# Cross-attention stack on one core: steps taken in pairs, a double piece after each, projection through a score pair, norm factors through DRAM

## The chip, the core and the metric

The kernel runs on one core of one Trainium2 chip. The time is the device time of one execution in microseconds. Before the change it was 5190.16 us, the median of three runs (5169.63 to 5191.87).

## What is computed

Four cross-attention layers, one after another, update the same 2048 rows of 256 numbers (`x`) from 1601 context rows of 512 (`ctx`). Layers 0, 2 and 3 are "masked": 16 heads of 64, with a bias on a few key columns that depends on the query row. Layer 1 is "grouped": 16 query heads of 16, four key heads, and an RMS norm ahead of it. All is float32.

```python
# masked layer
q, k, v = x @ Wq, ctx @ Wk, ctx @ Wv            # 16 heads of 64
logits = einsum('bhqd,bhkd->bhqk', q, k) * 64 ** -0.5
col_bias[:, token_indices_A] = -20 * (1 - mask_A)[:, None]
col_bias[:, token_indices_B] = -20 * (1 - mask_B)[:, None]
probs = softmax(logits + col_bias)
x = einsum('bhqk,bhkd->bhqd', probs, v) @ Wo + bo + x
# grouped layer
xn = x * rsqrt(mean(x * x) + 1e-5) * norm_w
q, k, v = xn @ wq, ctx @ wk, ctx @ wv           # 16 query heads, 4 key/value heads of 16
x = x + softmax(q k^T / 4) v @ wo
```

## The kernel before

**Blocks, units, chunks.** A masked layer has 8 blocks of two heads, the grouped layer 4 blocks of four heads that share one key head. A block is worked through for four query tiles of 512 rows; one query tile of one block is a unit, so there are 96 masked and 16 grouped units. The 1601 keys are cut into 13 chunks (`NT`): twelve of 128 and one of 65, the tail, in which the keys with a bias have been gathered.

**A masked unit.** For each chunk `masked_scores` (L662) multiplies the keys of both heads with the queries: two products of 64 rows, side by side in the array, into a score pair in PSUM (two banks). ScalarE copies the pair to an SBUF tile `p` (L680), VectorE keeps a running maximum `top` (L685, L683 for the second chunk). After the 13th chunk `maxima` (L721) transposes `top` on TensorE (L728), reduces it (L729), writes the result to DRAM and reads it back onto all partitions (`spread`, two DMAs of `on_all_partitions`, L630); `maxima_spread` (L741) copies it into the PSUM tile `b` (L744). Then, chunk by chunk, VectorE subtracts it (L749), ScalarE takes the exponential (L754), GpSimd adds it up over the chunks (L757, L759), and `values` (L779) multiplies by the values of both heads, into 64 columns each, and adds up in the one bank `po` (L794). After the last chunk `po` is copied to `oT` (L799). `denominators` (L805) transposes the sums (L815), reduces (L819), inverts (L820) and sends them over DRAM onto all partitions (`by`); `divide` (L834) multiplies `oT` by it on GpSimd; `project` (L837) multiplies by the output weights, one half of the 256 columns at a time, through the bank `pm`, and adds to `xs` (L846; L844 in a layer's last block, with the bias).

**PSUM** has eight banks: `po`, `pm` (one buffer each), two score pairs, and the pair `b`. In the grouped layer the three pairs are six single banks `t`.

**Pipeline by steps.** A step scores one chunk of one unit. The exponentials of a unit begin `DELAY` = 4 steps after its last score, its values follow one step (`LAG`) behind them. `p` has `NP` = 21 buffers. The loop at L978 writes out each step in order: subtraction (L749) of the older unit, scores and copy and maximum of the younger, exponential, (at the first step of a unit) the maxima of the one before, values of the older. The order of the program's instructions on TensorE, ScalarE and VectorE is fixed as written (L1055 to L1061); SyncE issues the DMAs in its own order, with waits.

**Pieces.** Work for later units and blocks is put between steps. `Pieces.step` (L902) first runs what is due at the step: the queries of the next unit (two halves of 256 columns, due at its steps 7 and 8, L428), `denominators` 2 steps, `divide` 5 steps, the two halves of `project` 7 and 8 steps after the last values of the unit. Then, as far as a credit of TensorE time allows, it takes pieces from a queue: the keys and the values of the next block, one chunk a piece (L398 and L409), each four products over the 512 context columns into `pm`, and a copy by ScalarE (L407, L418). The context comes as slices of two chunks (`context_slice`, L237).

**Grouped layer.** Row maxima are found from scores with the queries as columns (L699), the scores are computed a second time (L764) and go into the exponential; four heads of 32 rows at a time. `norm_factors` (L580) computes the RMS factors of a query tile and sends them through a DRAM tile onto all partitions of a constant tile `factors`, which the queries are multiplied by (L561).

Of the kernel before, what the change touches and what calls it, by code (L numbers as in the profile page):

```python
# [18 lines left out]
P = 128  # L19
QB = 512  # L20
# [5 lines left out]
Piece = namedtuple("Piece", "run cost")  # L26
# [7 lines left out]
def tile_cross_attention_stack(ctx: ExitStack, tc: tile.TileContext, t: dict, out: bass.AP):  # L34

# [43 lines left out]
    NP = 21  # L79
# [156 lines left out]

    def context_slice(c, held):  # L237

        a = TCH[c][0]
        n = sum(m for _, m in TCH[c : c + 2])  # L240
        ct = work.tile([P, NCT, 2 * P], FP, name="ct", bufs=3)
        nc.sync.dma_start(out=ct[:, :, :n], in_=ctxT_dram[:, :, a : a + n])
        for d in range(len(TCH[c : c + 2])):
            held[c + d] = lambda k, d=d: ct[:, k, d * P : (d + 1) * P]

    def first_context_slice(i):
# [21 lines left out]
        return lambda c, k: tiles[k // 2][:, k % 2, TCH[c][0] - a0 : TCH[c][0] - a0 + P]  # L268
# [93 lines left out]
    factors = const.tile([P, NB, QB], FP, name="factors")  # L362
# [5 lines left out]
    class Masked:  # L368
# [26 lines left out]
        def projections(self, u):  # L395


            def keys(c, ct):  # L398
                if u.kT is None:
                    u.kT = heads.tile([P, T], FP, name="kT")  # L400
                a, m = TCH[c]
                pk = ps_m.tile([P, QB], FP, name="pm")[:, :m]
                for k in range(NCT):
                    nc.tensor.matmul(  # L404
                        pk, u.wk[:, k, :], ct(k)[:, :m], start=(k == 0), stop=(k == NCT - 1)
                    )
                nc.scalar.copy(u.kT[:, a : a + m], pk)  # L407

            def values(c, ct):  # L409
                if u.v is None:  # L410
                    u.v = heads.tile([P, NT, P], FP, name="v")
                m = TCH[c][1]
                pv = ps_m.tile([P, QB], FP, name="pm")[:m, :P]
                for k in range(NCT):
                    nc.tensor.matmul(  # L415
                        pv, ct(k)[:, :m], u.wv[:, k, :], start=(k == 0), stop=(k == NCT - 1)
                    )
                nc.scalar.copy(u.v[:m, c, :], pv)  # L418
# [9 lines left out]
        def query_pieces(self, unit):  # L428

            xt = unit.transposed_x()  # L430
            half = QB // 2

            def queries(j):
                if j == 0:
                    unit.q = heads.tile([P, QB], FP, name="q", bufs=3)
                part = ts(j, half)
                pq = ps_m.tile([P, QB], FP, name="pm")[:, :half]
                for k in range(NC):
                    nc.tensor.matmul(  # L439
                        pq, unit.u.wq[:, k, :], xt[:, k, part], start=(k == 0), stop=(k == NC - 1)  # L440
                    )
                nc.scalar.mul(unit.q[:, part], pq, 64 ** -0.5)

            return [(7 + j, Piece(lambda j=j: queries(j), 1.0)) for j in range(2)]
# [650 lines left out]
```

## Time and profile before

| | |
|---|---|
| runs | 5169.63, 5190.16, 5191.87 us |
| profiled execution | 5180.84 us, of which the span of instructions 5179.1 us |
| mean granted TensorE clock | 0.983 |
| largest groups (busy us, mean ns) | POOL sums L759 2729.1, 2369; PE values L794 1631.5, 534; DVE subtraction L749 1505.8, 1207; PE scores L668 1414.1, 643; ACT exponential L754 1322.0, 1059; DVE maximum L685 1291.4, 1223; ACT copy L680 1263.1, 1012 |
| pieces on PE (busy us, mean ns) | keys L404 346.7, 288; values L415 344.7, 287; projection L840 257.6, 657; queries L439 189.9, 405; transposes L815 119.2, 301 and L728 118.3, 297 |
| DMA | 64 GB/s over the span, 22.5% of the engines on the main queue |

The profiler records single instructions of one execution. Lines are those of the kernel before. Records of matmuls on one engine overlap, because a matmul's end is modelled and the next one starts while it still runs: for TensorE the distance from one start to the next is what counts, not the length of a record. A float32 product appears as two matmul records (two passes), and two heads that run side by side in the array start within a few nanoseconds of each other.

### The profile page before, as it was taken

To read this page: it belongs to the slowest core of one execution; us is meant where nothing else is said; L and a number is where in the kernel's file an instruction comes from. 1 tells how busy PE (TensorE), PEld (TensorE's weight loads), DVE (VectorE), ACT (ScalarE), POOL (GpSimd) and SP (SyncE) were. 2 spreads that over 40 slices of the span, in tenths; PEclk is the share of its full clock that TensorE was granted. 3 is DMA by queue.
4 is the path that set the end of the run, shared out by engine and by line. 5 is a ranking of instruction groups with operands and counts; after the bars stand their busy time and mean duration, and the time that the engine had idled before them with its cause. 6 is when DMAs were issued, how large, how long until landed. Compare 5 with 4: busy or idle time off the path is not lost.

```text
span 5179.1 us, 67967 instructions
## 1 busy us (share of the span) xinstructions
PE 4983.5 (96%) x25652; PEld 2135.9 (41%) x25652; DVE 3755.4 (73%) x3887; ACT 3321.7 (64%) x4398; POOL 2997.5 (58%) x1429
## 2 busy tenths in 40 slices
PE   6899999999999999999999999999999999999997
PEld 4344444344444444454344343443444443443432
DVE  3777777777775666653577777777777777778786
ACT  2677776777635555544667777767677777777674
POOL 1677777777730000000477777777777777777777
PEclk9999999999989999999999999999999999999998
DMA  4122222222211000011122222222222222222211
GB/s 130 52 84 76 75 79 74 80 73 80 63 39 29 14 16 20 14 39 45 57 81 77 79 74 78 75 79 74 75 82 74 79 74 78 75 79 74 76 32 33
DMA packets 350823, 334.98 MB, mean 65 GB/s; under 512 B 120505, under 2 KB 306105, under 8 KB 350496
## 3 DMA queue, kind: packets, MB, share of 16 engines
q1 hardware_dynamic: 347232, 325.27, 22.5%
q8 instruction: 202, 3.31, 0.3%
q0 software_dynamic: 1152, 3.28, 0.2%
q10 hardware_dynamic: 2112, 2.10, 0.1%
q14 instruction: 125, 1.02, 0.1%
HBM read 315.75 MB, written 14.82 MB: 64 GB/s over the span
## 4 chain that ended last, share of the span: by engine, by line
PE 83%; ACT 8%; DVE 6%; issue 1%; DMA 1%; POOL 0%; ACTq 0%; SPq 0%; POOLq 0%; DVEq 0%
PE po L794 23%; PE s L668 23%; PE t L699 7%; PE pm L415 6%; PE pm L404 6%; ACT p L680 5%; PE pm L840 4%; PE pm L439 4%; DVE top L685 3%; PE t L764 3%; ACT p L754 3%; PE s L728 2%; DVE p L749 1%; PE pm L824 1%; PE pm L557 1%
## 5 line engine op out<-in xcount | busy, mean ns | idle before, releaser
L759 POOL TENSOR_TENSOR sums<-sums,p 128x1024 f32<-128x1024 f32 (+1 forms) x1152 | 2729.1, 2369 | 861.5 <-ACT p L754 756.8
L680 ACT COPY p<-s 128x1024 f32<-128x1024 f32 (+1 forms) x1248 | 1263.1, 1012 | 1018.3 <-PE s L668 868.9
L685 DVE TENSOR_TENSOR top<-s,top 128x1024 f32<-128x1024 f32 (+1 forms) x1056 | 1291.4, 1223 | 649.4 <-ACT p L680 648.7
L794 PE MATMUL po<-p,v 128*64 128x512 f32 (+3 forms) x8320 | 1631.5, 534 | 50.1 <-ACT oT L799 24.2
L749 DVE TENSOR_TENSOR p<-p,b 128x1024 f32<-128x1024 f32 (+1 forms) x1248 | 1505.8, 1207 | 72.0 <-ACT b L744 71.0
L668 PE MATMUL s<-q,kT 64*128 64x512 f32 (+1 forms) x4992 | 1414.1, 643 | 26.6 <-DVE top L685 26.3
L754 ACT ACTIVATE p<-p 128x1024 f32<-128x1024 f32 (+1 forms) x1248 | 1322.0, 1059 | 134.6 <-DVE p L749 129.6
L794 PEld LDWEIGHTS po<-p,v 128*64 128x64 f32 (+3 forms) x8320 | 315.5, 125 | 1201.4 <-issue 484.7
L776 ACT ACTIVATE p<-t 128x512 f32<-128x512 f32 (+1 forms) x764 | 414.6, 594 | 418.9 <-PE t L699 365.4
L712 DVE TENSOR_REDUCE row_top<-t 128x1 f32<-128x512 f32 x704 | 453.6, 686 | 262.7 <-PE t L699 257.8
L835 POOL TENSOR_TENSOR oT<-oT,by 128x512 f32<-128x512 f32 x112 | 143.0, 1277 | 861.3 <-DMA by<-cols 458.8
L668 PEld LDWEIGHTS s<-q,kT 64*128 64x128 f32 (+1 forms) x4992 | 368.9, 181 | 488.3 <-issue 218.3
L699 PE MATMUL t<-kT,q 32*128 32x512 f32 (+1 forms) x1888 | 557.8, 634 | 0.1
L764 PE MATMUL t<-q,kT 32*128 32x512 f32 (+1 forms) x1528 | 487.6, 652 | 0.0
L404 PEld LDWEIGHTS pm<-ct,wk 128*128 128x128 f32 x2392 | 290.8, 192 | 242.2 <-issue 191.0
L415 PEld LDWEIGHTS pm<-wv,ct 128*128 128x128 f32 (+1 forms) x2392 | 286.6, 187 | 250.5 <-issue 172.5
L415 PE MATMUL pm<-wv,ct 128*128 128x128 f32 (+1 forms) x2392 | 344.7, 287 | 34.1 <-DVE xs L846 20.6
L699 PEld LDWEIGHTS t<-kT,q 32*128 32x128 f32 x1888 | 296.1, 316 | 160.5 <-issue 81.9
L404 PE MATMUL pm<-ct,wk 128*128 128x128 f32 (+1 forms) x2392 | 346.7, 288 | 8.4 <-ACT kT L407 5.4
L840 PE MATMUL pm<-oT,wo 128*128 128x512 f32 x448 | 257.6, 657 | 13.0 <-POOL oT L835 12.1
L757 POOL COPY sums<-p 128x1024 f32<-128x1024 f32 x96 | 99.6, 1038 | 241.3 <-ACT p L754 241.3
L439 PE MATMUL pm<-xT,wq 128*128 128x256 f32 x672 | 189.9, 405 | 0.0
(153 smaller groups left out, 2449.6 us busy)
## 6 DMA issues: line engine op xcount, KB each, us to landing
ct<-ctxT SPq DMA_DIRECT2D x288, 512.0 KB
xT<-xT SPq DMA_DIRECT2D x100, 512.0 KB
spread<-cols SPq DMA_DIRECT2D x96, 512.0 KB
by<-cols SPq DMA_DIRECT2D x192, 128.0 KB
xT<-xs SPq DMA_DIRECT2D x16, 512.0 KB
ct<-ctxT SPq DMA_DIRECT2D x48, 130.0 KB
wk<-in_L_xattn_Wk_dram SPq DMA_DIRECT2D x24, 256.0 KB
wv<-in_L_xattn_Wv_dram SPq DMA_DIRECT2D x24, 256.0 KB
```

Source lines behind the costliest of these rows:

```text
L404: nc.tensor.matmul(pk, u.wk[:, k, :], ct(k)[:, :m], start=(k == 0), stop=(k == NCT - 1))
L415: nc.tensor.matmul(pv, ct(k)[:, :m], u.wv[:, k, :], start=(k == 0), stop=(k == NCT - 1))
L668: nc.tensor.matmul(s[:m, h, :], self.u.kT[r, a : a + m], self.q[r, :], start=True, stop=(a != TAIL),)
L680: nc.scalar.copy(p[:m], s[:m])
L685: nc.vector.tensor_tensor(self.top[:m], s[:m], self.top[:m], ALU.max)
L699: nc.tensor.matmul(s[:, at : at + n], self.q[r, columns(q)], self.u.kT[r, a : a + n], start=True, stop=True,)
L749: nc.vector.tensor_tensor(self.p[c][:m], self.p[c][:m], self.less[:m], ALU.add)
L754: nc.scalar.activation(p[:m], p[:m], AF.Exp)
L759: nc.gpsimd.tensor_tensor(self.sums[:m], self.sums[:m], p[:m], ALU.add)
L764: nc.tensor.matmul(s[:m], self.u.kT[r, a : a + m], self.q[r, :], start=True, stop=True)
L794: nc.tensor.matmul(to, v, p, start=(c == 0 and not part), stop=(c == NT - 1 and part != 0))
L840: nc.tensor.matmul(py, self.u.wo[:, ts(k, P)], self.oT, start=True, stop=True)
```

## The change

- The loop takes two steps at a time. In masked layers a pair writes both subtractions, both scores (with copies and maxima), both exponentials, both values, and then the pieces. Where the first step of a pair ends a unit's values, its values go ahead of the exponentials, and those of the next unit's first chunk go behind the pieces. `DELAY` is 5 and `LAG` 2 instead of 4 and 1, `NP` 22 instead of 21. Grouped steps are still written one by one.
- Pieces have double size: keys of two chunks in one product of 256 columns, values of two chunks in one bank and one copy, queries of 512 columns. At most one piece that uses `pm` (`shared`) is run per pair.
- `project` does both halves at once through a score pair (two single banks in the grouped layer), 8 steps after the last values, with one addition of 1024 wide, except in a layer's last block. `denominators` comes 3 steps after them instead of 2 (1 in the grouped layer).
- `maxima` is written at the end of the pair that has the unit's last scores, instead of in the next unit's first step.
- `factors` is a DRAM tile; each grouped unit reads its 512 factors onto all partitions when its queries are planned.

```diff
-Piece = namedtuple("Piece", "run cost")
+Piece = namedtuple("Piece", "run cost shared", defaults=(True,))
...
-    NP = 21
+    NP = 22
...
-    factors = const.tile([P, NB, QB], FP, name="factors")
+    factors = dram.tile([NB, P, QT], FP, name="factors")
+    def two_values(v, wv, c, ct):
+        f = wv.shape[2]
+        chunks = TCH[c : c + 2]
+        m = chunks[0][1]
+        pv = ps_m.tile([P, QB // P, P], FP, name="pm")
+        for d, (_, md) in enumerate(chunks):
+            for k in range(NCT):
+                nc.tensor.matmul(
+                    pv[:md, d, :f], ct(k)[:, d * P : d * P + md], wv[:, k, :],
+                    start=(k == 0), stop=(k == NCT - 1),
+                )
+        nc.scalar.copy(v[:m, c : c + len(chunks), :], pv[:m, : len(chunks), :f])
...
-                a, m = TCH[c]
-                pk = ps_m.tile([P, QB], FP, name="pm")[:, :m]
+                a, n = TCH[c][0], width(c)
+                pk = ps_m.tile([P, QB], FP, name="pm")[:, :n]
                 for k in range(NCT):
-                    nc.tensor.matmul(
-                        pk, u.wk[:, k, :], ct(k)[:, :m], start=(k == 0), stop=(k == NCT - 1)
-                    )
-                nc.scalar.copy(u.kT[:, a : a + m], pk)
+                    nc.tensor.matmul(pk, u.wk[:, k, :], ct(k), start=(k == 0), stop=(k == NCT - 1))
+                nc.scalar.copy(u.kT[:, a : a + n], pk)
...
-            half = QB // 2
-            def queries(j):
-                if j == 0:
-                    unit.q = heads.tile([P, QB], FP, name="q", bufs=3)
-                part = ts(j, half)
-                pq = ps_m.tile([P, QB], FP, name="pm")[:, :half]
+            def queries():
+                unit.q = heads.tile([P, QB], FP, name="q", bufs=3)
+                pq = ps_m.tile([P, QB], FP, name="pm")
                 for k in range(NC):
                     nc.tensor.matmul(
-                        pq, unit.u.wq[:, k, :], xt[:, k, part], start=(k == 0), stop=(k == NC - 1)
+                        pq, unit.u.wq[:, k, :], xt[:, k, :], start=(k == 0), stop=(k == NC - 1)
                     )
-                nc.scalar.mul(unit.q[:, part], pq, 64 ** -0.5)
-            return [(7 + j, Piece(lambda j=j: queries(j), 1.0)) for j in range(2)]
+                nc.scalar.mul(unit.q, pq, 64 ** -0.5)
+            return [(7, Piece(queries, 2.0))]
...
+            factor = work.tile([P, QB], FP, name="factor")
+            src = factors[unit.b].rearrange("p q -> (p q)").rearrange("(o n) -> o n", o=1)
+            nc.sync.dma_start(out=factor, in_=src.to_broadcast((P, QB)))
...
-            on_all_partitions(by, [(factors[:, b, :], slice(0, 1))])
+            with nc.allow_non_contiguous_dma(reason="512 values, four at a time"):
+                nc.sync.dma_start(out=factors[b], in_=by)
...
-        def project(self, k):
-            py = ps_m.tile([P, QB], FP, name="pm")
-            nc.tensor.matmul(py, self.u.wo[:, ts(k, P)], self.oT, start=True, stop=True)
-            to = xs[:, self.b, k, :]
-            if self.masked and self.u.n == self.layer.BLOCKS - 1:
-                bo = bo_of[self.layer.l][:, k : k + 1]
-                nc.vector.scalar_tensor_tensor(to, py, bo, to, ALU.add, ALU.add)
-            else:
-                nc.vector.tensor_tensor(to, py, to, ALU.add)
+        def project(self):
+            k = 0
+            for py in psum.heads(False):
+                of = range(k, k + py.shape[1])
+                for k in of:
+                    nc.tensor.matmul(
+                        py[:, k - of[0], :], self.u.wo[:, ts(k, P)], self.oT, start=True, stop=True
+                    )
+                k += 1
+                if self.masked and self.u.n == self.layer.BLOCKS - 1:
+                    for j in of:
+                        bo, to = bo_of[self.layer.l][:, j : j + 1], xs[:, self.b, j, :]
+                        nc.vector.scalar_tensor_tensor(
+                            to, py[:, j - of[0], :], bo, to, ALU.add, ALU.add
+                        )
+                else:
+                    to = xs[:, self.b, of[0] : k, :]
+                    nc.vector.tensor_tensor(to, py, to, ALU.add)
         def finish(self):
-            found = [
-                (2 if self.masked else 1, Piece(self.denominators, 1.0)),
-                (5, Piece(self.divide, 0.0)),
+            return [
+                (3, Piece(self.denominators, 1.0, not self.masked)),
+                (5, Piece(self.divide, 0.0)), (8, Piece(self.project, 2.0, False)),
...
-        def step(self, step, share, cost):
-            self.credit = max(min(self.credit + share - cost, 1.5), -1.5)
-            for piece in self.due.pop(step, ()):
-                piece.run()
-                self.credit -= piece.cost
-            while self.fill and self.credit >= self.fill[0].cost / 2:
+        def steps(self, steps, share, cost):
+            self.credit = max(min(self.credit + share - cost, 2.5), -2.5)
+            taken = False
+            for step in steps:
+                for piece in self.due.pop(step, ()):
+                    piece.run()
+                    self.credit -= piece.cost
+                    taken |= piece.shared
+            while self.fill and not taken and self.credit + cost >= self.fill[0].cost / 2:
                 piece = self.fill.popleft()
                 piece.run()
                 self.credit -= piece.cost
+                taken = piece.shared
...
-            first = chunks(makers[0], lambda m: m / P)
-            second = chunks(makers[1], lambda m: 1.0)
+            first = chunks(makers[0], lambda c: width(c) / P)
+            second = chunks(makers[1], lambda c: float(len(TCH[c : c + 2])))
...
-    DELAY, LAG = 4, 1
+    DELAY, LAG = 5, 2
...
+    for first in range(0, N + NT + DELAY + LAG + 16, 2):
+        pair = [Step(first), Step(first + 1)]
+        if any(masked(x.scoring) for x in pair):
+            if psum.banks:
+                psum.by_pairs()
+        elif pair[0].exping and not pair[0].exping.masked and not psum.banks:
+            psum.singly()
+        kn, cn = divmod(first + 2 - NT - DELAY, NT)
+        ahead = of[kn] if cn == 0 and 0 <= kn < len(units) and of[kn].masked else None
+        three = not ahead and not any(masked(x.exping) for x in pair)
+        for x in pair:
+            x.begin()
+        if first == 4:
+            token_rows()
+        for x in pair:
+            if masked(x.exping):
+                if x.cb == 0 and x is pair[1]:
+                    x.exping.maxima_spread()
+                x.exping.subtract(x.cb)
+        for x in pair:
+            if masked(x.scoring):
+                x.scoring.masked_scores(x.ca)
+        ends = all(masked(x.valuing) for x in pair) and pair[0].cv == NT - 1
+        if ends:
+            pair[0].valuing.values(NT - 1)
+        for x in pair:
+            if masked(x.exping):
+                x.exping.masked_exp(x.cb)
+        if ahead:
+            ahead.maxima_spread()
+        if not ends:
+            for x in pair:
+                if masked(x.valuing):
+                    x.valuing.values(x.cv)
+        together = [pair] if masked(pair[0].scoring) and masked(pair[1].exping) else [pair[:1], pair[1:]]
+        for some in together:
+            for x in some:
+                x.grouped(three)
+                x.end()
+            shares = [x.share() for x in some]
+            pieces.steps([x.step for x in some], *map(sum, zip(*shares)))
+        if ends:
+            pair[1].valuing.values(0)
+        for x in pair:
+            if x.scoring and x.ca == NT - 1:
+                x.scoring.maxima()
```

`begin`, `end`, `share` and `grouped` of the new class `Step` hold what the loop did before at the start of a unit, at its sixth step and last values, for the credit, and for a grouped step.

## The prediction

> **What bounds the kernel now.** I read the page first (busy time), then the busy time by stretch over one block of a masked layer, then the order of time on TensorE, then who waited for whom.
>
> ```profile
> PE 4983.5 (96%) x25652; PEld 2135.9 (41%) x25652; DVE 3755.4 (73%) x3887; ACT 3321.7 (64%) x4398; POOL 2997.5 (58%) x1429
> ```
>
> ```profile
> 834.00:1000.40 166.40, 163.35 (x746) 67.15 (x744) 131.81 (x121) 117.42 (x146) 122.22 (x57) 1.00 0.27 77
> ```
>
> The second fence is the stretch of one masked block (four units, 52 steps; columns: us, then PE, PEld, DVE, ACT, POOL busy, clock, DMA). TensorE is busy 163.35 of 166.40 us; DVE 79%, POOL 73%, ACT 71%. So TensorE sets the time, and what matters is what its busy time consists of:
>
> ```profile
> 998.40 1.16 PE L404 MATMUL pm<-ct,wk 128*128 128x128 f32 x8
> 999.49 1.13 PE L668 MATMUL s<-q,kT 64*128 64x512 f32 x4
> 1000.55 1.08 PE L794 MATMUL po<-p,v 128*64 128x512 f32 x4
> 1001.56 1.12 PE L840 MATMUL pm<-oT,wo 128*128 128x512 f32 x2
> 1002.62 1.08 PE L668 MATMUL s<-q,kT 64*65 64x512 f32 x4
> ```
>
> ```profile
> 5131.69 1.10 PE L794 MATMUL po<-p,v 128*64 128x512 f32 x4
> 5132.19 1.03 PE L794 MATMUL po<-p,v 128*64 128x512 f32 x4
> 5132.62 1.02 PE L794 MATMUL po<-p,v 128*64 128x512 f32 x4
> 5133.05 1.02 PE L794 MATMUL po<-p,v 128*64 128x512 f32 x4
> ```
>
> Read start to start, since ends overlap. A step is scores on 64 rows (S), values into 64 columns (V), a piece on the full array (F): 1.06 + 1.01 + 1.06 = 3.13 us. The second fence is the kernel's tail, where two chunks of values follow one another with nothing between: the passes start 0.43 us apart. Each S, V and 512-wide F is two passes (two heads side by side count once), 0.86 us of streaming. So 3.13 us holds 2.58 us of streaming; 0.55 us is lost at three changes of shape.
>
> ```profile
> PE s L668 <- DVE top L685: 26.3, 94, 2.2
> PE po L794 <- ACT oT L799: 24.2, 25, 3.6
> PE pm L415 <- DVE xs L846: 20.6, 22, 1.0
> ```
>
> TensorE's longest waits for others (us in total, times, longest) are small.
>
> **Part 1: half the changes of shape.** From the single records (medians): in S the first pass takes 533 ns and the last, up to the V behind it, 526, against 430 in a stream: 103 + 96 = 199 ns a run. V: 480 and 529, so 50 + 99 = 149. F: keys 213 first, 112 in stream, 205 last; L840 533 and 522 against 430: about 194. The issue orders of the two programs, counted in unbroken runs of one shape, give for the masked layers S 1228 to 613, V 1221 to 658, F 1092 to 549. Saved: 615 x 0.199 + 563 x 0.149 + 543 x 0.194 = 122 + 84 + 105 = 312 us. The grouped layer keeps its order inside a step; only pieces merge (109 to 69 F runs) and 16 other runs go: 10 us. Together 322. Streaming itself is unchanged: the same columns pass.
>
> The price needs the second chunk's weights to load under the first chunk's streaming. The tail shows that for V (0.43 us across the chunk boundary), the key pieces for F (112 ns apart, while a load of L404 lasts 192 ns on average). For S there is one pair of neighbours in the prologue, near 114 us, 430 ns apart. I take the full price.
>
> The Trainium skill speaks against it: "TensorE: Matmul & The Clock Gate", Part 3, section "The mechanism" (what overlaps and what doesn't), says that a weight load overlaps running matmuls only when its row group differs. Both chunks use the same rows, so by it no entry would be saved; the key pieces' 112 ns under 192 ns loads disagree. It is rival B.
>
> **Part 2: waits of TensorE that go.** (a) Values one step behind the exponential (LAG 1), and V of a unit's first chunk behind the oT copy: 144 of 1024 S-to-V gaps are longer than 526 ns, together 43.6 us; LAG 2 and the split of V at a unit's end remove them. (b) L815's transposes to the next S: 537 ns instead of 205, 92 times: 30 us, for the score pair whose row maximum is not done; in a pair of steps V, V stand between. (c) L840 to a value piece in the same step: 1535 ns instead of 522, 23 times: 23 us, one pm buffer; the projection leaves pm. (d) Pieces waiting for pm to be copied: 15. Sum 112; I take 105, bounds 60 and 112.
>
> **Part 3: waits that come.** The projection takes a score pair, so a unit asks 16 times for one of two pairs instead of 15, and DVE's order in a pair of steps is fixed: two subtractions (L749, 1.207 each), two maxima (L685, 1.223 each), then the piece's work. One pair of steps streams S, S, V, V in 1.92 + 1.87 us. From the rows:
> - After the projection: its last pass ends 0.59 after its start, the 1024-wide add takes about 1.22 (as L685 does), with 0.06 for semaphores 1.87. The second S of the next pair wants that buffer at 0.52 + 0.96 = 1.48. Wait 0.4, every unit.
> - After L728's transposes (0.30 for the last, L729 1.225, 0.06: 1.58) the second S of the next pair comes at 0.21 + 0.96 = 1.17: 0.4, in units whose last chunk stands first in its pair, and likewise after L815's (L819 1.215) in the others.
> - The projection falls in the pair after the maxima, wants the first S's buffer: reduction until 1.58, two subtractions, one maximum: 5.2. TensorE gets there at 0.21 + 1.92 + 0.4 + 1.87 = 4.4: 0.8, in the first kind of unit.
> - In the other kind no shared piece stands ahead of the transposes, and `top` is late: DVE takes L819 and L820 until 1.7 after the transposes of the denominators, then 2.41 + 2.45: 6.6. TensorE arrives at 0.2 + 1.92 + 0.4 + 0.4 (tail keys) + 1.87 = 4.8: 1.8.
>
> Units of the first kind: 0.4 + 0.8 + 0.4 = 1.6; of the second: 0.4 + 1.8 + 0.4 = 2.6; mean 2.1, over 96 masked units 204 us. Behind the waiting S stand the pair's V and piece; ACT waits for the same S. Bounds: 0, if DVE runs ahead, and 408, if each wait pushes DVE back once more.
>
> **At nothing.** The sums on POOL, the exponentials and the copies: a masked block should take 166.4 - (312 + 105 - 204) / 24 = about 157.5 us, and DVE's 132, POOL's 122, ACT's 117 fit below. If DVE didn't fit, that is rival C. The maxima issue their two DMAs at the end of the pair, not a step into the next unit; before, ntop to L744's copy had 10.5 us and L744 waited 2.8 us in all for them; two pairs give 11.5. Norm factors through DRAM: 16 reads more on SP's queue, each asked for a pair ahead of use, where before the broadcast went the same way over DRAM; the cover is the grouped unit's own scores; without it some 5 us four times. Prologue: fewer waits for pm (L415 for L407 9.7, L404 for L418 3.2 us) against two steps more of POOL (2.37 each) in the tail: 0, give or take 8.
>
> **Sum** against the profiled execution, 5180.84 us (span 5179.1; runs shown 5169.63 to 5191.87, median 5190.16, which is 0.2% above it): 5180.8 - 322 - 105 + 204 = 4958, say 4955.
>
> **Rivals.**
> A. The new waits are hidden: 4958 - 204 = 4754; half of them, 4856. For: DVE idles 20% of a block. Against: the order in a pair is written out, and DVE can't take the next subtraction early.
> B. Loads of the second chunk don't hide: entries of S and V stay, 615 x 0.103 + 563 x 0.050 = 91: 5049. Against: V's 0.43.
> C. Twice the new waits, DVE being 84% used and never early: 5162.
> D. Slower. The 22 buffers for p are just what is alive: 20 steps from copy to value, in pairs 22; before 19 of 21. The copy of the scores (L680) then waits for POOL's sum of the chunk 22 steps back. POOL ends the two sums of a pair 4.25 + 4.74 = 9.0 after the pair begins, 3.0 into the next one, and the copy comes 1.2 into the one after it: 4.2 us of slack. POOL is in order, and behind the divide (1.28) it idles for the reciprocals' way over DRAM:
>
> ```profile
> POOL oT L835 <- DMA by<-cols: 458.8, 83, 68.6
> ```
>
> 5.5 us a time on the average. The denominators now come at step 3 instead of 2, the divide stays at 5. If POOL waited 5.5 every unit, 5.5 + 1.28 - 4.2 = 2.6 us a unit would reach ACT, then S: 96 x 2.6 = 250 us, 5208; if it waited the longest way I find in the records (6.9 us from L820's end to L835; most are 5.3 to 5.8) 4.0 and 5340; say 5250. It turns slower from a wait of 5.2, where 2.3 us a unit eat the 223. Against: a pair lasts 5.7 us, so the rows come mostly in time; L680 waited 12.8 us for POOL in all.
> That the change doesn't do what it says is ruled out by the issue orders, which show the runs.
>
> **Chances.** Forecast (4890 to 5025) 0.68; A 0.10; B 0.07; C (5080 to 5165) 0.09; D 0.06. The range 4855 to 5075 holds the forecast, half of A and B: 0.80. Faster by over 0.5% (about what a measurement of this kernel tells from no change; the runs differ by 0.4%) 0.91, within 0.03, slower 0.06.
>
> **What would show it.** Start to start in a pair: S, S 1.92, V, V 1.87, key piece 1.93; a masked block near 157.5 us; TensorE's waits led by L735 and L850 (the new lines of the transposes and the projection) for DVE's maxima, and S for L862 and L736, about 0.4 us each. S to S at 533 would be B; ACT's copy waiting for POOL's sums some hundred us would be D; DVE over 90% of a block C. I am wrong if the block stays above 163 us or falls below 152.

## The result and the profile after

| | before | after |
|---|---|---|
| median of the runs | 5181.29 us (4 runs) | 5004.29 us (4 runs, 4995.41 to 5006.5) |
| ratio | | 0.9656, 95% interval 0.9627 to 0.9685 |
| the same kernel again, in a later comparison | 5177.79 (9 runs) | 4991.67 (5 runs), 0.9645, 0.9631 to 0.9659 |
| profiled execution: span, granted clock | 5179.1, 0.983 | 4993.7, 0.977 |

The page's busy times of the changed kernel (from here on, line numbers are those of the changed kernel, if not said otherwise):

```profile
PE 4713.8 (94%) x24004; PEld 2064.5 (41%) x24004; DVE 3755.6 (75%) x3782; ACT 3214.5 (64%) x4000; POOL 2991.6 (60%) x1429
```

TensorE is busy 270 us less; VectorE (DVE) exactly as long as before. A pair of steps on TensorE, from the order of time (start, duration, line):

```profile
3616.40 1.95 PE L381 MATMUL pm<-wv,ct 128*128 128x128 f32 x16
3618.28 1.99 PE L675 MATMUL s<-q,kT 64*128 64x512 f32 x8
3620.20 1.94 PE L801 MATMUL po<-p,v 128*64 128x512 f32 x8
3622.06 1.08 PE L675 MATMUL s<-q,kT 64*65 64x512 f32 x4
```

Start to start, scores of two chunks take 1.92 us, values of two chunks 1.86, the piece of double size 1.88. One masked block, unit by unit, between the maxima transposes (columns: us, then PE, PEld, DVE, ACT, POOL busy, clock, DMA share, GB/s):

```profile
3078.30:3115.00 36.70, 34.31 (x148) 13.97 (x146) 31.81 (x28) 26.50 (x31) 31.60 (x15) 1.00 0.30 84
3115.00:3156.74 41.74, 41.23 (x203) 18.71 (x204) 34.16 (x30) 30.06 (x34) 29.58 (x15) 1.00 0.30 83
3156.74:3193.56 36.82, 33.80 (x156) 13.84 (x155) 31.81 (x28) 26.32 (x30) 32.03 (x15) 1.00 0.25 66
3193.56:3235.40 41.84, 41.58 (x179) 18.08 (x180) 34.10 (x30) 30.21 (x35) 29.09 (x15) 1.00 0.35 91
```

The four add up to 157.10 us (median over 14 blocks 157.1), where a block took 166.4 before. Units now alternate: a *short* one (six pairs between its transposes; its last chunk stands second in its pair) of 36.8 us, and a *long* one (seven pairs; last chunk first) of 41.8. In the long one TensorE is busy all but 0.3 to 0.5 us, in the short one it idles 2.4 to 3.0. The waits of TensorE (total, times, longest):

```profile
PE s L735 <- DVE top L692: 75.7, 52, 1.8
PE s L675 <- DVE top L692: 22.9, 46, 1.6
PE s L675 <- DVE xs L862: 22.0, 85, 0.3
PE s L675 <- DVE ntop L736: 18.6, 72, 0.3
PE s L850 <- DVE top L690: 18.5, 38, 0.5
```

Before, scores waited for the maximum too (26.3 us) and the maxima transposes next to nothing (0.9 us); the other three are new. The first is at the end of every short unit, seen in the order of time of all engines:

```profile
3111.61 1.94 PE L801 MATMUL po<-p,v 128*64 128x512 f32 x8
3112.34 2.54 DVE L692 TENSOR_TENSOR top<-s,top 128x1024 f32<-128x1024 f32 x2
...
3114.94 1.23 PE L735 MATMUL s<-ident,top 128*128 128x128 f32 x8 [1.39 <-DVE top L692]
```

The last values are done at about 3113.5; the last two maxima end at 3114.88, so the transposes wait 1.39 us for them.

The list counts a wait from the modelled end of the record before. That end lies behind the point at which the next pass could have started, so the list shows less than a wait costs. A pair of scores whose second chunk waits for its bank:

```profile
3086.04 1.13 PE L675 MATMUL s<-q,kT 64*128 64x512 f32 x4
3087.43 1.13 PE L675 MATMUL s<-q,kT 64*128 64x512 f32 x4 [0.26 <-DVE xs L862]
3088.49 1.94 PE L801 MATMUL po<-p,v 128*64 128x512 f32 x8
```

It takes 2.45 us where an undisturbed pair takes 1.92: 0.53 us lost, and 0.26 of it counted. By the single records (medians over 14 blocks) the second chunk starts 854 ns behind the pass before instead of 429, and the pass after it starts 533 ns later, as behind a change of shape, instead of 429. This happens in 116 of 364 pairs of scores (in the short last chunk the second figure is 481), 4.4 us a block in all.

Where the 185 us of span went, from the starts of the transposes of the n-th masked unit:

| stretch | before | after | difference | by the forecast |
|---|---|---|---|---|
| start to unit 4 | 303.1 | 290.1 | -13.0 | -9 |
| units 4 to 28 (six blocks of layer 0) | 995.7 | 943.9 | -51.8 | -53 |
| units 28 to 36 (last block, grouped layer, first block) | 1371.6 | 1373.0 | +1.4 | -28 |
| units 36 to 92 (fourteen blocks) | 2325.9 | 2199.4 | -126.5 | -125 |
| unit 92 to the end | 182.9 | 187.4 | +4.5 | -9 |

The last column spreads the sum on record: 8.9 us a block and 10 in the grouped layer. The first row also moves from one execution to the next: the changed kernel's second profile began its first scores at 69.3 us instead of 78.5 and had 279.1 there.

Inside the third row, the body of the grouped layer fell from 889.3 to 877.9 us. Its entry and its exit grew (first scores to first second scores; last scores to last second scores). Before, then after:

```profile
1433.20:1513.70 80.50, 73.11 (x284) 31.51 (x282) 61.08 (x62) 25.96 (x27) 38.29 (x18) 0.79 0.16 46
...
2403.10:2500.80 97.70, 92.16 (x520) 28.64 (x519) 23.39 (x24) 53.89 (x57) 1.27 (x1) 0.90 0.11 33
```

```profile
1362.70:1455.60 92.90, 84.81 (x302) 34.91 (x300) 65.58 (x64) 26.23 (x28) 41.55 (x19) 0.74 0.15 47
...
2333.40:2444.20 110.80, 101.30 (x560) 32.47 (x560) 26.76 (x25) 55.54 (x59) 1.26 (x1) 0.88 0.11 34
```

Entry +12.4, exit +13.1 us. The entry holds 18 and the exit 40 TensorE instructions more, as `DELAY` puts the second scores one step later. Both also ran at a lower granted clock (0.74 against 0.79, 0.88 against 0.90).

### The profile page after: what moved, and what is told of

It is laid out like the page before. It is cut to its first block, busy times and chain, and to the rows that moved or that the text cites. A ratio compares the mean times of both kernels' runs of the same rounds, so it can differ in the third digit from the quotient of the medians.

```text
span 4993.7 us, 64038 instructions
## 1 busy us (share of the span) xinstructions
PE 4713.8 (94%) x24004; PEld 2064.5 (41%) x24004; DVE 3755.6 (75%) x3782; ACT 3214.5 (64%) x4000; POOL 2991.6 (60%) x1429
## 3 DMA queue, kind: packets, MB, share of 16 engines
q1 hardware_dynamic: 348960, 328.41, 23.9%
## 4 chain that ended last, share of the span: by engine, by line
PE 78%; DVE 14%; issue 2%; DMA 2%; POOL 1%; ACT 1%; SPq 0%; another core or an unknown queue 0%; POOLq 0%; DVEq 0%; ACTq 0%
PE po L801 23%; PE s L675 17%; PE t L706 8%; PE pm L381 6%; PE pm L427 5%; DVE p L756 5%; PE s L850 4%; PE pm L451 4%; DVE top L692 3%; PE t L771 3%; PE s L822 2%; DVE xs L862 2%; PE s L735 2%; POOL sums L766 1%; DVE rden L826 1%
## 5 line engine op out<-in xcount | busy, mean ns | idle before, releaser
L687 ACT COPY p<-s 128x1024 f32<-128x1024 f32 (+1 forms) x1248 | 1227.8, 1014 | 744.3 <-PE s L675 693.7
L756 DVE TENSOR_TENSOR p<-p,b 128x1024 f32<-128x1024 f32 (+1 forms) x1248 | 1461.1, 1209 | 77.9 <-ACT b L751 77.9
L801 PE MATMUL po<-p,v 128*64 128x512 f32 (+3 forms) x8320 | 1509.0, 530 | 8.8 <-ACT p L761 7.7
L675 PE MATMUL s<-q,kT 64*128 64x512 f32 (+1 forms) x4992 | 1318.2, 629 | 73.0 <-DVE top L692 22.9
L761 ACT ACTIVATE p<-p 128x1024 f32<-128x1024 f32 (+1 forms) x1248 | 1255.8, 1059 | 55.1 <-DVE p L756 54.0
L801 PEld LDWEIGHTS po<-p,v 128*64 128x64 f32 (+3 forms) x8320 | 367.3, 126 | 1120.6 <-issue 835.1
L381 PE MATMUL pm<-wv,ct 128*128 128x128 f32 (+2 forms) x2496 | 320.0, 281 | 10.6 <-DMA ct<-ctxT 4.9
L427 PE MATMUL pm<-ct,wk 128*128 128x256 f32 (+1 forms) x1288 | 296.7, 373 | 1.3 <-DMA wk<-in_L_xattn_Wk_dram 0.8
L427 PEld LDWEIGHTS pm<-ct,wk 128*128 128x128 f32 x1288 | 221.8, 191 | 115.9 <-issue 57.1
L736 DVE TENSOR_REDUCE ntop<-s 128x8 f32<-128x1024 f32 x96 | 117.5, 1224 | 188.9 <-PE s L735 188.9
L850 PE MATMUL s<-oT,wo 128*128 128x512 f32 x392 | 196.6, 624 | 41.5 <-DVE top L690 18.5
L764 POOL COPY sums<-p 128x1024 f32<-128x1024 f32 x96 | 99.5, 1036 | 157.5 <-ACT p L761 157.2
```

What stands on the lines that cost most here:

```text
L381: nc.tensor.matmul(pv[:md, d, :f], ct(k)[:, d * P : d * P + md], wv[:, k, :], start=(k == 0), stop=(k == NCT - 1),)
L427: nc.tensor.matmul(pk, u.wk[:, k, :], ct(k), start=(k == 0), stop=(k == NCT - 1))
L675: nc.tensor.matmul(s[:m, h, :], self.u.kT[r, a : a + m], self.q[r, :], start=True, stop=(a != TAIL),)
L687: nc.scalar.copy(p[:m], s[:m])
L756: nc.vector.tensor_tensor(self.p[c][:m], self.p[c][:m], self.less[:m], ALU.add)
L761: nc.scalar.activation(p[:m], p[:m], AF.Exp)
```

## The experiments

Diffs are against the changed kernel. A block is the median of 14 masked blocks. Ratios are to the kernel before, run beside each.

**Steps taken apart again (e2).**

```diff
         for x in pair:
             if masked(x.scoring):
                 x.scoring.masked_scores(x.ca)
+            if masked(x.valuing) and not (ends and x is pair[1]):
+                x.valuing.values(x.cv)
...
-        if not ends:
-            for x in pair:
-                if masked(x.valuing):
-                    x.valuing.values(x.cv)
```

> The changed kernel with the two chunks of a pair taken apart again: scores, values, scores, values, and then the piece of double size; the lag of two steps, the projection through a score pair and the factors by DRAM stay. Theory (the gain comes from fewer changes of shape on TensorE): scores runs go from about 613 to 1228 and values runs from 658 to 1221; at 199 and 149 ns a run that is 122 + 84 = 206 us of TensorE work more, of which part takes the place of waits for DVE that the pairs brought (up to 150 us): 5060 to 5200 us, a block of masked attention at 160 to 165.7 us instead of 157.1, neighbours of unlike shape still 526 to 533 ns apart. Rival (the gain came from the double pieces and the longer lag, not from the pairs): within 20 us of 5004.

5101.51 us, 0.9853 (0.9838 to 0.9868), block 162.13. The theory holds, in the lower part of its range. A block has 52 runs of scores instead of 26 and 52 of values instead of 28; at 199 and 149 ns a run that is 8.7 us, and the block takes 5.0 us more. The price of a run is as forecast: start to start (medians over 14 blocks) a first score takes 533 ns, scores to values 526, a first value 480, values to scores 529, against 429 in a stream, 348 ns for a run of each. What comes off is the 4.4 us that waiting second chunks cost the pairs: here no second chunk follows, and no score run waits inside. 8.7 less 4.4 is 4.3; the remaining 0.7 is not explained. L735 waits 76.6 us here too: the pairs of scores and values are not what makes that wait.

**Key and value pieces of single size (e9).**

```diff
+                a, n = (TCH[c][0], width(c)) if d is None else TCH[c + d]
...
+                    Piece(lambda c=c, d=d: piece(c, d), TCH[c + d][1] / P if make is makers[0] else 1.0)
+                    for c in range(0, NT, 2) for d in range(len(TCH[c : c + 2]))
...
+        if all(masked(x.scoring) for x in pair) and masked(pair[1].exping):
+            pieces.between()
```

> The changed kernel with the key and value pieces of masked layers in single size again, one of them at most behind the scores and one behind the values of a pair; the loads of the context, the pairs and all else stay. By the written order a block then has some 38 runs of the full array instead of 26. Theory (a run of the full array costs 0.19 us whatever its length): 12 x 23 x 0.194 = 54 us more: 5058 us, 5035 to 5080, neighbours in a key piece still 0.11 us apart. Rival (single pieces spread better over the pairs, and cover waits for DVE as large as what they cost): within 15 us of 5004.

5069.68 us, 0.9775 (0.9760 to 0.9790), block 160.0. The theory holds: 36.0 runs of the full array a block instead of 23.7, and 2.9 us more, 0.24 us a run (by the mean of the blocks, which a few long ones raise, 3.4 us and 0.28). TensorE's waits, counted start to start, are as long as in the changed kernel (8.0 and 8.1 us a block).

**The projection's halves through pm (e4).**

```diff
-            for py in psum.heads(False):
...
+            for k in range(NC):
+                py = ps_m.tile([P, QB], FP, name="pm")
+                nc.tensor.matmul(py, self.u.wo[:, ts(k, P)], self.oT, start=True, stop=True)
```

> The changed kernel with the output projection's two halves one after another through the single bank pm again, as before the change, instead of through a score pair. Theory (the score pair only trades waits): the waits of scores runs for the projection's add (22.0 us) and of the projection for the maximum of the chunk before (18.5) go, and the second half waits about 0.9 us for the add of the first in each of 96 projections, 86 us: about +45, 5050 us. Rival (the score pair costs more than it gives, as the projection takes one of two pairs from the scores): about -40, 4965 us, the long unit of a block shorter than 41.8 us.

5073.70 us, 0.9803 (0.9788 to 0.9818). The first waits of TensorE in this kernel:

```profile
PE pm L848 <- DVE xs L854: 99.1, 100, 1.6
PE s L735 <- DVE top L692: 75.8, 52, 1.8
```

The theory holds: the second half's wait came, with the last blocks' form of the addition (13.4) 112.5 us in all, the grouped layer's included, and the 40.5 us of the pair's waits went. The difference of 72 is near what the time shows: 69 to 82 us by the two medians of the changed kernel, 61 to 65 by the profiled executions, from which the waits are. That is more than the 45 forecast, which had 86 for the second half's waits. The score pair gives more than it costs.

**A lag of one step (e6), and with it the distances of before (e8).**

```diff
-    DELAY, LAG = 5, 2
+    DELAY, LAG = 6, 1
```

This is e6; e8 has 4 and 1.

> The changed kernel with the exponentials one step nearer to the values: DELAY 6 and LAG 1 instead of 5 and 2, so that scores and values stay as far apart and stand in the same places. The second chunk's values of a pair then need the exponential of the same pair's first. Theory (the longer lag is what takes TensorE's waits for ACT away): by the timeline of the changed kernel that exponential ends about 1.1 us after those values could start; waits of values for ACT appear in most pairs, 0.3 to 1.0 us in each of some 600, 180 to 600 us: 5300 us, 5150 to 5600. Rival (the lag isn't needed in pairs): within 30 us of 5004, values waiting for ACT less than 60 us in all.

> The changed kernel with the distances of before, DELAY 4 and LAG 1, so that a unit's values come two steps earlier behind its scores. Theory for what the forecast missed (each entry into and exit from the grouped layer takes a grouped step longer on the average, as 80.5 us from its first scores to its first second scores became 92.9, and 97.7 at its end became 110.8): the stretch from the maxima of masked unit 28 to those of unit 36, 1373.0 us in the changed kernel, is shorter by 20 to 25 us than that of the run with DELAY 6 and LAG 1, whatever the lag costs in the masked blocks. Rival (the half clock or the blocks around it make it): within 8 us of that run's. The time: 5250, 5050 to 5550, by the waits of values for ACT.

e6: 5917.48 us, 1.1413 (1.1395 to 1.1430), block 197.7. e8: 5637.15 us, 1.0867 (1.0848 to 1.0884), block 183.5. TensorE's first wait in e6:

```profile
PE po L801 <- ACT p L761: 802.9, 572, 4.5
```

The cause is the expected one and the price larger: 1.4 us in nearly every pair. With one step of lag the kernel with pairs is 14% slower than the one before the change. On the grouped layer's edges e8 is between the two claims: units 28 to 36 take 1449.0 us against e6's 1460.0, with 12.1 us less at the entry and 3.9 at the exit for two steps. So distance does lengthen them, about 6 us a step at the entry. At the exit e8 had 45.6 us of half clock (stretches with a granted clock of 0.5) and e6 27.3, which hides part of the two steps. The neighbouring blocks differ by 14 us in these runs, so both figures are rough.

**Denominators a pair earlier (e1), and a piece at the end of every unit (e5).**

```diff
-                (3, Piece(self.denominators, 1.0, not self.masked)),
+                (2 if self.masked else 3, Piece(self.denominators, 1.0, not self.masked)),
```

```diff
-                (3, Piece(self.denominators, 1.0, not self.masked)),
-                (5, Piece(self.divide, 0.0)), (8, Piece(self.project, 2.0, False)),
+                (3, Piece(self.denominators, 1.0)),
+                (5, Piece(self.divide, 0.0, not self.masked)), (8, Piece(self.project, 2.0, False)),
...
-                spent = 1.0 if self.scoring.masked and self.ca == NT - 1 else 0.0
+                spent = 0.0
```

The first is e1, the second e5.

> The changed kernel with one number changed: the denominators of a masked unit are due 2 steps after its last values instead of 3. In units whose last chunk is the second of its pair this moves their transposes (L822) one pair earlier, into the pair with the query piece. Theory (the wait of the maxima transposes for DVE's running maximum, 75.7 us in all, comes from DVE being late because the reduce of the denominators, and the projection's add behind it, fall into the last pairs of the unit): that wait falls to about 15, the long unit of a block from 41.8 to about 40.3 us, and the time by about 50: 4945 us, 4930 to 4965. Rival (DVE has simply too much to do in that unit, so that the wait only moves to scores runs and projections): within 10 us of the changed kernel's 5004, the sum of TensorE's waits for DVE unchanged.

> The changed kernel with only the place of the pieces moved: the division on POOL no longer counts as a piece that bars a key or value piece from its pair, the denominators do, and the maxima are charged nothing. By the written order every unit then ends with a key or value piece between its last values and its maxima transposes (except in a layer's last block), and the pair of the denominators has none; no run of one shape is added. Theory (the transposes of the maxima wait 1.45 us in units whose last chunk stands second in its pair, because nothing stands between the last values and them): the 75.7 us of L735's waits fall below 15, those units take 35.4 instead of 36.8 us, a block 154 instead of 157.1, the time falls by about 60: 4945 us, 4925 to 4965. Rival (DVE is behind by as much whatever stands there, so the wait turns up at the scores of the pair that lost its piece): within 15 us of 5004, the sum of TensorE's waits for DVE unchanged.

e1: 5003.34 us, 0.9667 (0.9654 to 0.9681), block 158.6. e5: 5012.78, 0.9663 (0.9650 to 0.9676), block 158.1. Both theories fall. TensorE's waits for the maxima, the first two lines of each list (e1, then e5):

```profile
PE s L735 <- DVE top L692: 74.7, 52, 1.6
PE s L675 <- DVE top L692: 41.1, 87, 2.3
...
PE s L735 <- DVE top L692: 39.0, 48, 1.8
PE s L675 <- DVE top L692: 23.7, 45, 3.5
```

In e1 the transposes moved in the short units, L735 still waits 74.7 us, and 18 more turn up at the scores. In e5 L735's wait fell to 39.0 us, the scores' wait for the denominators (L826) rose from 6.1 to 23.4, and the short unit takes 36.7 us as before. Its long units have a run of the full array more (25.6 a block instead of 23.7), which the expectation had not counted. Moving TensorE's work within a short unit does not shorten it.

**More work for VectorE (e10).**

```diff
             nc.vector.tensor_tensor(self.p[c][:m], self.p[c][:m], self.less[:m], ALU.add)
+            if c == 6:
+                nc.vector.tensor_reduce(spare, self.less, AX.X, ALU.max)
```

> The changed kernel with one more instruction on VectorE in each of the 96 masked units, behind the subtraction of chunk 6: a maximum over the 1024 columns of the spread maxima into a tile that nothing reads (about 1.22 us by the rows of the other reductions). Theory (units whose last chunk stands second in its pair, 36.7 us with DVE 31.8 busy and waiting 5 for answers, are set by DVE; the others, 41.7 us with TensorE 41.2 busy, by TensorE): the former grow by 1.0 to 1.3 us, the latter by less than 0.5, a block from 157.1 to 159.5 to 160, the time by 55 to 75: 5070 us. Rival A (TensorE sets both kinds, and the wait of L735 is the length of one chain from the last scores): within 15 us of 5004. Rival B (DVE sets both): +4.8 us a block, 5115.

5125.33 us, 0.9902 (0.9881 to 0.9923), block 163.6. Short units grew by 1.1 us, as expected of units that DVE sets; long ones by 1.85 to 2.4, more than the 1.22 us added. The busy time around the end of one short unit, in slices, shows why:

```profile
3255.00:3258.00 3.00, 1.15 (x9) 1.15 (x10) 1.70 (x2) 0.43 (x1) 2.92 (x2) 1.00 0.28 82
3258.10:3261.50 3.40, 3.40 (x14) 2.05 (x14) 3.38 (x3) 0.26 (x1) 2.21 (x2) 0.52 0.17 50
3261.50:3265.00 3.50, 3.50 (x16) 1.12 (x13) 1.32 (x2) 3.35 (x4) 0.28 (x1) 0.98 0.82 151
```

TensorE waits 2.89 us at L736 (this kernel's transposes), and the next 3.4 us run at about half clock (0.52). Of the 40 long units in the table's twenty blocks, 37 have such a stretch; the three without take 42.66 us, 0.9 above the 41.8 of the changed kernel. So VectorE's order sets the short units, and the long ones nearly as much: rival A falls. By the time rival B (5115) comes nearest; without the half clock the long units' 0.9 lies between the theory (under 0.5) and rival B (the whole 1.22). So a part of the 121 us is the clock.

**The pieces balanced between the units (e11).**

```diff
-            while self.fill and not taken and self.credit + cost >= self.fill[0].cost / 2:
+            while self.fill and not taken and at not in (5, 11) and (
+                at in (4, 6, 10, 12) or self.credit + cost >= self.fill[0].cost / 2
+            ):
```

Here `at` is the chunk that the pair's second step scores; even ones belong to short units. The division bars no piece, as in e5.

> The changed kernel with the same number of key and value pieces, but four instead of three in the units whose last chunk stands second in its pair (the new one between the last values and the maxima transposes, where TensorE waits 1.45 us) and three instead of four in the others; by the written order a block has no run of the full array more than before. Theory (the former are set by DVE and have room on TensorE, the latter by TensorE): the long units fall from 41.8 by 1.2 (a key piece and its change of shape) or 2.2 us (a value piece), the short ones stay within 0.5 us of 36.8, a block falls from 157.1 to about 154.2, the time by about 65: 4940 us, 4920 to 4965. Rival (DVE's work and waits set both kinds, so that only the waits move, as the run that gave every unit a piece at its end showed): a block within 1 us of 157.1, 4990 to 5020.

4970.57 us, 0.9600 (0.9583 to 0.9617), block 155.85. Two units, short and long:

```profile
3067.24:3104.32 37.08, 36.08 (x156) 15.39 (x155) 31.90 (x28) 26.56 (x31) 29.98 (x14) 1.00 0.28 81
3104.32:3145.13 40.81, 39.50 (x188) 16.68 (x188) 34.06 (x30) 30.19 (x35) 31.51 (x15) 1.00 0.30 86
```

Half of the theory: the short units took a whole piece for 0.4 us, but the long ones fell only to 40.8, the same whether a key piece (1.0 us) or a value piece (2.0) had gone. There TensorE now idles 1.3 us: VectorE sets them too. L735's wait fell to 10.9 us, that of scores for the maxima rose from 22.9 to 63.5.

**The grouped denominators in one product (e7).**

```diff
-                for q in range(QT):
-                    nc.tensor.matmul(
-                        pd[:, q, :], self.oT[:, columns(q)], den_rows, start=True, stop=True
-                    )
-                nc.vector.reciprocal(rden, pd.rearrange("p q h -> p h q"))
+                nc.tensor.matmul(pd, den_full, self.oT, start=True, stop=True)
+                nc.vector.reciprocal(self.by, pd)
+                return
```

> The changed kernel with the grouped layer's denominators made by one product of oT with a 128x128 matrix of zeros and ones, which leaves each head's denominator on all of its 32 partitions, and a reciprocal of that into the tile by; the four products of 4 columns each and the round trip by DMA that spread their result go. Theory (the stretches of 3.4 us at half clock in the grouped layer, 11 in nine units after the change against 5 before, follow the 2.03 us of 4-column products): they fall below 5 in nine units, the mean granted clock of that stretch rises from .96 to .98 or more, and with L831's 2.03 us becoming about 0.96 the time falls by 16 x 1.07 + about 18 = 34: 4970 us. Rival (the half clock comes from the 32-row scores themselves, whatever the denominators do): the stretches stay, and only about 16 us go: 4988.

4978.71 us, 0.9617 (0.9604 to 0.9630). In the grouped body the stretches of half clock fell from 17 (61.4 us) to 4 (23.9 us). Of the 17, 13 began within 2 us of the thin products, those of 4 columns; of the 4 none begins within 13 us of the product that stands in their place. The busy time after, then in e7:

```profile
1460.00:2330.00 870.00, 869.22 (x6755) 422.87 (x6750) 506.79 (x827) 428.93 (x794) 24.91 (x32) 0.96 0.10 27
```

```profile
1450.00:2315.00 865.00, 864.22 (x6683) 417.29 (x6680) 547.76 (x829) 433.31 (x799) 24.91 (x32) 0.99 0.08 23
```

So the thin products do bring the half clock. But the body fell only from 877.9 to 870.5 us. The reciprocal now works on 512 columns; among the costliest groups of VectorE:

```profile
L837 DVE RECIPROCAL by<-pm 128x512 f32<-128x512 f32 x14 | 47.0, 3358 | 9.4 <-PE pm L835 8.8 <-issue 0.7
```

3.36 us, 16 times, on the engine that the grouped scores' banks wait for. That it gives back the rest of the gain is likely, not shown.

**Both edits together (e12), beside the changed kernel again.**

> The pieces balanced between the two kinds of units (4971 us by itself, .9600 of before) and the grouped layer's denominators by one product with a 128x128 matrix (4979 us, .9617) together. If the two parts don't touch each other, the gains against the changed kernel (.9656 of before) add: .9656 - .0056 - .0039 = .9561, 4955 us, 4940 to 4975; the grouped body near 870 us with few stretches of half clock, a masked block at 155.9 us. Rival (the gain of one of the two was the state of that run's chip): .958 to .962, 4965 to 4985.

> The changed kernel once more, unaltered, beside the run with both edits on the same chip. Theory: .9656 of before again within .0025, so that what the single edits were measured against holds; the combination is faster by 0.7 to 1.2%. Rival (the ratio moves from chip to chip): outside .963 to .968.

4966.01 us, 0.9593 (0.9578 to 0.9607), and 4991.67 us, 0.9645 (0.9631 to 0.9659). The combination is faster than the changed kernel beside it, by 0.5%; but the gains don't add: .9561 was the sum, and even counted from .9645 it would be .9572. The time lies where the rival had it. Both parts are there in the profile (a block of 155.9 us as in e11, a grouped body of 872.1 us with 23.9 us of half clock as in e7), so that a part of a single edit's gain was that of its own runs is likely, not shown. The changed kernel repeats within 0.0011.

## Why the prediction was right

4955 us was forecast, 5004 measured (4995.41 in the profiled execution, against a sum of 4958); faster, as given 0.91. The theory behind it is confirmed where it was made, in the masked blocks, and missed the grouped layer's edges.

1. *Half the changes of shape, 312 us.* Right: the runs halved as counted, and neighbours of one shape start 429 ns apart, scores and values alike, across the chunk boundary. That settles rival B, by which the second chunk's first pass would have taken 533 ns again; it does so only behind a wait. The prices held too: e2's records give 199 and 149 ns again for scores and values, and by e9 a full-array run costs 0.24 us, somewhat more than 0.194. With these prices the 26, 24 and 23 runs saved in a block make 14.3 us; the forecast had 13.0.
2. *Waits that go, 105 us.* Too high. Start to start, the waits of the kernel before come to 3.9 us a block, of which some 3.1 went; the forecast had 4.4. Values and pieces still wait a little (7.7 us for exponentials, 19.6 before), and scores for the maximum in other places (22.9 us, 26.3 before). e6 shows what the second step of lag is worth in pairs (0.8 ms of waits), e4 the score pair (some 70 us).
3. *Waits that come, 204 us.* Right in place, each of the four, and nearly in size. The list has 75.7 us for L735, 18.5 for the projection, 22.0, 18.6 and 6.1 for scores, together 141. But the forecast was worked out start to start, and so counted a wait of scores costs 0.43 us (0.4 forecast), one of the maxima transposes 1.5 (1.8), one of the projection 0.56 (0.8): 177 us, and with some 18 for the slow pass behind each waiting second chunk 195. The forecast had no term for that pass.
4. *The block.* 157.5 forecast, 157.1 measured. That it is so near is in part luck: the runs saved some 1.3 us a block more than priced, the waits that went some 1.3 less, and the two cancel (14.3 + 3.1 - 8.1 = 9.3 us net, as measured; 8.9 forecast).
5. *The step that failed* is the grouped layer's term of 10 us: the sum has nothing for that layer's edges, and of the longer distance it counts only "two steps more of POOL (2.37 each) in the tail". The body did give 11 us, but between units 28 and 36 the kernel came out 29 us behind the forecast: 12 at the entry, 13 at the exit, 5 in the blocks around, 1 better in the body. `DELAY` 5 makes entry and exit a step longer. At the entry e6 and e8 give about 6 us for a step. The half clock took more there: 47.8 us of it instead of 34.2 at the entry, 27.3 instead of 20.5 at the exit. In e1 the entry, in the same order, had 27.3 us of half clock and took 85.4 instead of 92.9 us, so some 0.37 us are lost by each us of it: an estimate of 5.0 and 2.5 us. At that rate e8's longer half clock hid 6.8 us at its exit, so that a step is worth some 5 us there as well. Steps and clock together explain some 18 us; 5 at the exit, the 5 in the blocks around and a little at the entry stay open.
6. The last block and the tail are 13 us behind the forecast: with no pieces for a next block, the block has only pairs of scores and values, 3.8 us on TensorE against 4.87 for the two subtractions and two maxima on DVE, and there is little for a saved change of shape to shorten. The last block's units fit (37.9 us on average after, 36.7 before); no run tests it alone, so this cause is argued, not shown.
7. *Rivals.* A (4754 or 4856): e10 and e11 show why not; DVE's order is what the block now runs up against. C (twice the waits): DVE is busy 84% of a block, and the waits came once. D: the copy of the scores (L687) waits 21.3 us for POOL's sums, 12.8 before, far from some hundred.

## What to carry to other kernels

Count runs of one shape, not matmuls: here each run of 64-row, 64-column or full-array products costs 0.15 to 0.24 us whatever its length. A wait inside a run breaks it: the pass behind is as slow as behind a change of shape, and start to start the wait costs twice what the list of waits shows (0.53 us against 0.26). Putting two chunks in one run needs their data a step earlier, so lengthen the lag with it (without that step this kernel was 14% slower). Once TensorE stops being the only limit, an instruction added to the next engine in line costs nearly its full length in the units that it sets (1.1 of 1.22 us here); look at the busy time unit by unit, since a block's average hides which unit belongs to which engine, and then move work between units, not within one.

## What the runs showed of the hardware

- *A pause shorter than a clock window can halve TensorE's clock.* In the masked blocks of 14 profiles, of 1093 gaps of 1.4 to 2.0 us between two matmul starts one was followed by a stretch of half clock within 5.2 us of its start; of 183 gaps of 2.0 to 2.6 us 21; of 3 between 2.6 and 2.9 us one; of 79 of 2.9 us or more 71. A gap holds the pass that it begins with, about 0.5 us. The stretches last 3.413 us or a multiple. The Trainium skill, "TensorE: Matmul & The Clock Gate", Part 1, "What's actually happening", gives the same window of 3413 ns, running freely, and says that the clock halves after at least one idle window; by these runs a gap of two thirds of a window can do, and one of 2.9 us mostly does. So from a gap of 2 us on, a wait can cost more than its length.
- *Idle time isn't needed for it.* In the grouped layer's body TensorE was busy 869 of 870 us, and of its 17 stretches of half clock 13 began within 2 us of the products of 4 columns (2.03 us for 8 of them). In e7, with those gone, 4 stretches were left.
- *Loads behind the same rows overlap.* Scores of two chunks use the same rows of the array and follow 429 ns apart, as in a stream. The Trainium skill, same page, Part 3, "The mechanism", has loads overlap with running matmuls only where the row group differs; here they overlap without that.
